# A planned FFN kernel on one core: transfers counted on a shared way, another order of the first loads, and the last pair's products in an order of their own

## The chip, the core and the metric

The kernel runs on one core of a Trainium2 chip. The metric is the device time of one execution in microseconds (us). A core has TensorE (PE, matrix products), VectorE (DVE), ScalarE (ACT), GpSimd (POOL) and SyncE (SP, which issues transfers here). Products accumulate in PSUM banks; everything else lies in SBUF. Every engine works through its own queue in the order in which its instructions were issued, and a semaphore makes it wait for another engine or a transfer.

## The reference, cut to what matters

```python
# x [64,64,1024], itok [64], cond weights [16,64,64]
W = weights[condition]                       # one 64x64 matrix per batch item
y = jnp.einsum('bct,bcd->bdt', x, W)         # mixes the 64 channels of an item
...
gate_logits = jnp.einsum('bsd,ed->bse', y, gate_w)          # 8 experts
weights, selected = jax.lax.top_k(gate_logits, 2)           # then softmax of the two
result = jnp.einsum('bsd,od->bso', y, base_w) + base_b      # 1024 -> 1024
low = jnp.einsum('bsd,erd->ebsr', y, lora_A)                # rank 16 for each expert
lora_out = jnp.einsum('ebsr,eor,bse->bso', low, lora_B, w_full)
result = result + 2.0 * lora_out
x = x + result
```

All values are float32.

## The kernel before, in words

There are 4,096 rows of 1,024 features, cut into 32 tiles of 128 rows (two batch items each). Mixing the channels acts on rows and the linear layers act on columns, so the kernel does the wide product first. It computes z = x * [lora_A | gate | base], 1,160 columns as three blocks of 388 (one padded), and then multiplies z from the left by the block-diagonal 128x128 matrix of the tile's two items. These second products are the `sums` (L431), into banks `ps_a` and `ps_o`.

Precision comes from splitting. Every f32 operand becomes a rounded high part (a CAST, L223, on ScalarE where nothing else is said) and a low part (operand minus high part, on VectorE, L220). A product of a row tile with one column block over 256 features is two halves of three matmuls (high x high, high x low, low x high), 128x388 each (`zstep`, L399).

The 16 pairs of row tiles come in two kinds. The first two (`NPLAIN`) run plainly: 24 products a pair (2 tiles x 3 column blocks x 4 stretches of features). The other 14 use a scheme with 20 products, p1 to p20, in the manner of Strassen's. Sums of x tiles (`sum_x`, L280) and of weight blocks (`mix_w`, L330) are formed once by VectorE, and then fewer products are needed. The products go to four banks, X, Y, R and Q (`ps_z0` to `ps_z3`); `BANK` (L61) says which. Partial results pass between them. `pass_on` (L690) is a ScalarE copy from one bank to another, times +1 or -1. `mix` (L707) is a VectorE add of a bank to a stored partial result `st`. p14, p15, p2, p8 and p9 all go to Y one after the other, and a mix stands after most of them.

When a chunk (one tile, one column block) of z is complete it is split (`zh`, `zl`), and `post` puts out the rest. For column block 0 this is the gate on the 8 logits, a transpose (L480) of the weighted low-rank part `low`, and its split `lth`/`ltl`. For all blocks it is the `sums`, with the matrix `bdr` gathered by POOL (L379) and with the LoRA products `lbh`, `lbl`. `finish` (L441) then adds to the token tile `xtok`, which holds x + bias. The token tile is loaded by SP (L365), and the bias is added by an accumulating transfer that POOL issues (L366). `store` writes it to memory, from POOL (L448), and for the last two tiles from SP (L450).

The order of nearly everything is planned. `Program.add` records a step with its engine, its cost and what it reads and writes. `Program.run` then lays the steps out greedily: on the engine that is free first, the ready step whose latest allowed start (`late`) is smallest. What it issues is in this planned order, on each engine. The planner knows hand-over times (`HOP`, `SAME`), when each engine may begin (`START`), and times after a step until its result counts as there (`lag`). In the kernel before, a load costs its bytes at 270 GB/s on SP, and `XLAG`, `WLAG`, `GATHER` and constants of 2, 4 and 5 us are its lags. TensorE's products alone have a fixed order (`PLAIN`, then `ORDER` made of `HEAD` and `TAIL`), and due times from it.

At the start the first weight block `b11` comes in two halves on ScalarE's queue, outside the plan (L301). The other blocks (`load_w`, L313) and the x tiles (`load_x`, L265) come on SP's queue, and `SUMS` forms weight sums as soon as their blocks are there. `b13` to `b43` are third-column blocks. The LoRA matrix `lb` is loaded into `xtok[2]` and split at L571 and L572.

Of the kernel before, what the change touches and what calls it, by code (L numbers as in the profile page):

```python
# [20 lines left out]
P = 128  # L21
B, C, T = 64, 64, 1024
NCOND = 16
E, R = 8, 16
# [18 lines left out]

HOP = {PE: 0.2, ACT: 0.15, DVE: 0.15, POOL: 0.15, SP: 1.0}
SAME = {PE: 0.0, ACT: 0.1, DVE: 0.12, POOL: 0.1, SP: 1.0}
START = {PE: 0.0, ACT: 2.0, DVE: 0.8, POOL: 1.7, SP: 1.4}
GATHER = 8.0
XLAG, WLAG = 3.0, 2.0
DMA = 1 / 270e3
AHEAD = 10.0  # L50
# [14 lines left out]
TAIL = ("p14", "p15", "p2", "p8", "p9")  # L65

SPLITS = (("f6", "a11"), ("s", "f5"), ("f19", "a22"), ("f11", "f13"), ("f18", "a24"), ("f3", "f1"), ("a13", "f9"),
          ("r", "f15"), ("f2", "f8"))
# [3 lines left out]
class Program:  # L72
# [6 lines left out]

    def add(self, engine, cost, fn, reads=(), writes=(), due=None, first=False, lag=0.0, early=None, port=False):  # L80

        n = len(self.steps)
        engine, cost = (e if isinstance(e, (list, tuple)) else [e] for e in (engine, cost))
        deps = set()
        for b in list(reads) + list(writes):
            if b in self.writer:
                deps.add(self.writer[b])
        for b in writes:  # L90
            deps.update(self.readers.get(b, ()))
        for b in reads:
            self.readers.setdefault(b, []).append(n)
        for b in writes:
            self.writer[b], self.readers[b] = n, []
        deps.discard(n)
        self.steps.append(dict(eng=dict(zip(engine, cost)), fn=fn, deps=deps, first=first, lag=lag, port=port,
                               due=self.horizon if due is None else due,
                               early=SP in engine and not reads if early is None else early))

    def run(self):
# [17 lines left out]
        def offer(i):  # L119
            for e in steps[i]["eng"]:  # L120
                t = max([0.0] + [end[d] + hop(by[d], e) + steps[d]["lag"]
                                 for d in steps[i]["deps"]])
                if steps[i]["early"]:
                    t = max(t, late[i] - AHEAD)
                t += MARGIN if steps[i]["first"] else 0.0
                cand[e].add((i, t))

        for i in range(n):
            if not left[i]:
                offer(i)  # L130
        done, port = 0, 0.0
        while done < n:
# [11 lines left out]
            end[i], by[i] = t + steps[i]["eng"][e], e  # L144
            free[e] = end[i]
            if steps[i]["port"]:
                port = end[i]
# [10 lines left out]
def cond_ffn_kernel(ctx, tc, xT, x, idx, cw, wall, bias, lb, out):  # L158
# [103 lines left out]

    def load_x(i, k, u, lag=XLAG):

        add(SP, DMA * 8 * P * P, lambda e: nc.sync.dma_start(  # L265
            xr[:, u].rearrange("p (k n) -> p k n", k=2), xT[i][:, 2 * k:2 * k + 2]), writes=[("xr", u)], lag=lag)

# [29 lines left out]


    raw["b11"] = Block("w_b11")
    for f in range(2):  # L300
        nc.scalar.dma_start(raw["b11"].ap()[:, f:f + 1], wall[0][0][:, f:f + 1])  # L301
    begun = [True]
    warm = sb.tile([P, 8], F32, name="warm")
    nc.vector.memset(warm, 0.0)
    nc.scalar.activation(warm, warm, AF.Exp)

    def load_w(m):

        k, n = int(m[1]) - 1, int(m[2]) - 1
        begun = m in raw  # L310
        if not begun:
            raw[m] = Block(f"w_{m}")
        add(SP, DMA * 8 * P * W, lambda e, b=raw[m]: None if begun else nc.sync.dma_start(b.ap(), wall[k][n]),  # L313
            writes=raw[m].keys, early=False)

# [10 lines left out]
    def mix_w(o, a, b, f, over):  # L326

        x, y = raw[a], raw[b]
        raw[o] = r = raw.pop(over) if over else Block(f"w_{o}")
        add(DVE, tt_cost(2 * W), lambda e: nc.vector.tensor_tensor(r.ap(), x.ap(), y.ap(), f),  # L330
            [k for z in (x, y) if z is not r for k in z.keys], r.keys, port=True)

# [29 lines left out]
    def load_tok(i):  # L362
        j = i % 3
        keys = [("xtok", j, c) for c in range(3)]
        add(SP, DMA * 4 * T * P, lambda e: nc.sync.dma_start(xtok[j], x[i * P:(i + 1) * P, :]), writes=keys, lag=4.0)  # L365
        add(POOL, 1.1, lambda e: nc.gpsimd.dma_start(xtok[j], bias.broadcast_to([P, T]), accum_op=ALU.add),  # L366
            writes=keys, lag=5.0)

    def late_sum(i):

        j = i % 3
        for src in (x[i * P:(i + 1) * P, :], bias.broadcast_to([P, T])):
            add(POOL, 1.1, lambda e, src=src: nc.gpsimd.dma_start(xtok[j], src, accum_op=ALU.add),
                writes=[("xtok", j, c) for c in range(3)], lag=5.0)

    def load_cond(i):
# [4 lines left out]
            in_offset=bass.IndirectOffsetOnAxis(ap=rows[:, i:i + 1], axis=0)),  # L381
            ["rows"], [("bdr", j)], lag=GATHER, early=True)
        add(ACT, 0.28, lambda e: copy(e, bdh[j], bdr[j]), [("bdr", j)], [("bdh", j)])
# [33 lines left out]

    def sums(i, c, b, q=None, part=(), with_lora=False, start=False, stop=False, first=True):

# [7 lines left out]
        def f(e):  # L427
# [5 lines left out]
        add(PE, len(part) * mm_cost(n) + 3 * with_lora * mm_cost(s.stop - s.start), f, sorted(names, key=str), [b],  # L433
            first=first)

# [8 lines left out]
    def store(i, cs):  # L444
        o, j = slice(outs(cs[0])[1].start, outs(cs[-1])[1].stop), i % 3
        src = [("xtok", j, c) for c in cs]
        if i < NT - 2:
            add(POOL, 1.0, lambda e: nc.gpsimd.dma_start(out[i * P:(i + 1) * P, o], xtok[j][:, o]), src, lag=2.0)  # L448
        else:
            add(SP, 0.5, lambda e: nc.sync.dma_start(out[i * P:(i + 1) * P, o], xtok[j][:, o]), src)  # L450

# [25 lines left out]
    def tr(i, b):  # L477
# [3 lines left out]
                                                  stop=False, skip_group_check=True),  # L481
            [("low", i % 2), "ident"], [b], first=True)
        add(ACT, 0.25, lambda e: copy(e, h, tp), [b], [("lth", i % 2)])
# [4 lines left out]
    def post(i, c, q):  # L488
# [7 lines left out]
        else:  # L496
            b = f"o{take('o', 2)}"
            if (i, c) == (NT - 2, 2):
                sums(i, c, b, with_lora=True, start=True)
                sums(i, c, b, q, (0, 1), first=False)  # L500
                sums(i, c, b, q, (2,), stop=True, first=False)
            else:
                sums(i, c, b, q, (0, 1, 2), True, True, True)
# [7 lines left out]
    for q in range(1, NPLAIN):  # L511
        PLAIN += [(i, c, k) for c in range(3) for i in (2 * q, 2 * q + 1) for k in range(KQ)]
    t = 4.2
    for i, c, k in PLAIN:
# [5 lines left out]
    for q in range(NPLAIN, NPAIR):  # L520
        nxt = HEAD if q + 1 < NPAIR else ()
        mixed = ("p14", nxt[0:1], "p15", nxt[1:2], "p2", nxt[2:3], "p8", "p9", nxt[3:])
# [20 lines left out]
    def load_split_x(i, k, **how):  # L543
        u = xrs.one()
        load_x(i, k, u, 0.0)
        xa0[i, k], = split_x([u], **how)
        xrs.give(u)

    for k in range(KQ):
        for i in range(2):  # L550
            load_split_x(i, k, hi=DVE if i == k == 0 else ACT)
            load_split_w(f"b{k + 1}{i + 1}", step=1 if i == k == 0 else 2)

# [14 lines left out]
    lraw = [("xtok", 2, c) for c in range(3)]  # L568
    add(SP, DMA * 4 * T * P, lambda e: nc.sync.dma_start(xtok[2], lb), writes=lraw)

# [108 lines left out]
    class Pair:  # L679
        def __init__(self, q):  # L680
            self.q, self.ops, self.at = q, Operands(q), {}

# [25 lines left out]

        def chunk(self, i, c, o):
            u = self.at[o]  # L710
            post(2 * self.q + i, c, split_z(CN[c], lambda: unit(u)[:, :CN[c]], ukey(u)))
            sts.give(u)

        def product(self, p):
            q, j, b = self.q, self.ops.split(p), BANK[p]
            for f in range(2):
                zstep((q, p, f), BANKS[b], j, p, f, p in OPENS and f == 0, p in STOPS and f == 1)
            self.ops.done(p)
            minus = ALU.subtract
            if p == "p6":  # L720
# [12 lines left out]
            elif p == "p13":  # L733
                self.mix("c23", "R", "p6")
                sts.give(self.at["p6"])
            elif p == "p18":
# [8 lines left out]
            elif p == "p12":  # L745
                post(2 * q, 0, split_z(N0, lambda: bank[BANKS["X"]][:, :N0], BANKS["X"]))
            elif p == "p14":
                self.mix("c23", "Y", "c23")
                self.chunk(1, 2, "c23")
            elif p == "p15":  # L750
                self.mix("c22", "Y", "c22")
                self.chunk(1, 1, "c22")
                store(2 * q + 1, range(3))
            elif p == "p2":
                self.mix("c12", "Y", "c12")
                self.chunk(0, 1, "c12")
                if q == NPAIR - 1:
                    store(2 * q, (0, 1))
            elif p == "p9":
                self.mix("c13", "Y", "c13", minus)  # L760
                self.chunk(0, 2, "c13")
                store(2 * q, (2,) if q == NPAIR - 1 else range(3))

# [51 lines left out]
```

## Time and profile before

| | |
|---|---|
| median of 3 runs | 467.27 us (466.59 to 467.89) |
| the profiled execution | 467.18 us |
| its span, first to last instruction | 465.2 us |
| VectorE: splits (L220), x and weight sums, partial results | 387.6 us busy |
| TensorE's first product / its last one starts | 5.06 / 460.30 us |
| last add on VectorE ends | 461.24 us |
| bytes moved | 75.00 MB, 161 GB/s on average |

The span leaves out about 2.0 us of the execution that lie before its first and behind its last instruction. The groups of instructions that the change touches most are these:

```profile
L280 DVE TENSOR_TENSOR xr<-xr 128x256 f32<-128x256 f32 (+1 forms) x139 | 71.1, 527 | 3.9 <-DMA xr<-in_xT 3.6
...
L690 ACT ACTIVATE ps_z<-ps_z 128x388 f32<-128x388 f32 x42 | 20.1, 480 | 31.7 <-PE ps_z L399 28.5
...
xr<-in_xT SPq DMA_DIRECT2D x128, 128.0 KB, 3.4
...
xtok<-in_x SPq DMA_DIRECT2D x28, 512.0 KB, 4.6
```

A group's line gives the code line, the engine, the operation, output <- input and how often; then its busy time and the mean of one in ns; then how long the engine had been idle just before and who ended most of that. A line of a transfer gives KB each and the median time from issue to landing. In a timeline the first number is the start in us, the second the duration, and brackets hold the idle time before and its releaser.

### The profile page before, as it was taken

How to read it: one execution, taken by the hardware profiler on the slowest of the kernel's cores; microseconds unless marked ns; L12 is line 12 of the kernel's file. 1: busy time of each engine (PE TensorE's matmuls, PEld its weight loads, DVE VectorE, ACT ScalarE, POOL GpSimd, SP SyncE). 2: the span in 40 equal slices, each digit the busy share in tenths (PEclk: the TensorE clock that was granted, in tenths of full speed). 3: DMA queues.
4: the chain of work that ended last, by engine and by line, in shares of the span. 5: the costliest groups of instructions: out<-in, count | busy, mean ns of one | idle time of the engine just before them, and what ended most of it. 6: DMA issues, size and time to landing. Idle time of an engine off the chain costs nothing.

```text
span 465.2 us, 7574 instructions
## 1 busy us (share of the span) xinstructions
PE 455.1 (98%) x2615; PEld 449.3 (97%) x2615; DVE 387.6 (83%) x938; ACT 223.2 (48%) x520; POOL 90.4 (19%) x107
## 2 busy tenths in 40 slices
PE   7999999999999999999999999999999999999986
PEld 6999999899999999999999999999999999999975
DVE  5999997788888898797888988888888889798573
ACT  5665665463643536364361735436363443636340
POOL 4020202413112021211303021120302203203200
PEclk9999999999999999999999999999999999999999
DMA  8940846884746556483576456476454646657542
GB/s 291 308 131 25 146 126 136 233 205 150 195 156 183 126 185 145 143 196 99 197 160 192 126 165 163 132 190 188 141 144 152 167 112 182 155 194 167 128 126 90
DMA packets 35509, 75.00 MB, mean 161 GB/s; under 512 B 4352, under 2 KB 21136, under 8 KB 35472
## 3 DMA queue, kind: packets, MB, share of 16 engines
q0 software_dynamic: 10560, 36.72, 33.4%
q1 hardware_dynamic: 24624, 37.41, 24.6%
q10 hardware_dynamic: 288, 0.40, 0.3%
q8 instruction: 20, 0.33, 0.3%
q14 instruction: 17, 0.14, 0.1%
HBM read 57.74 MB, written 16.78 MB: 160 GB/s over the span
## 4 chain that ended last, share of the span: by engine, by line
PE 91%; DMA 4%; DVE 2%; ACT 1%; issue 1%; SPq 0%; ACTq 0%; DVEq 0%
PE ps_z L399 70%; PE ps_o L431 14%; PE ps_a L431 6%; DMA xr<-in_xT 3%; DMA w_b<-in_w 1%; PE ps_a L480 1%; DVE st L707 1%; DVE xr L280 1%; DVE xl L220 0%; ACT st L223 0%; DVE xtok L441 0%; DVE wl_b_b L220 0%; SPq L265 0%; ACT wh_t_p L223 0%; ACT wh_b_b L223 0%
## 5 line engine op out<-in xcount | busy, mean ns | idle before, releaser
L223 ACT CAST xh<-xr 128x512 fp32r<-128x512 f32 (+1 forms) x137 | 82.9, 608 | 65.9 <-PE ps_z L399 64.8
L399 PE MATMUL ps_z<-wh_t_p,xh 128*128 128x388 f32 x308 | 105.6, 343 | 1.4 <-DVE st L707 1.3
L399 PE MATMUL ps_z<-wh_t_p,xl 128*128 128x388 f32 x308 | 104.3, 339 | 0.0
L399 PE MATMUL ps_z<-wl_t_p,xh 128*128 128x388 f32 x308 | 104.3, 339 | 0.0
L220 DVE TENSOR_TENSOR xl<-xr,xh 128x512 fp32r<-128x512 f32 (+1 forms) x138 | 92.0, 670 | 11.3 <-ACT xh L223 10.8
L707 DVE TENSOR_TENSOR st<-ps_z,st 128x388 f32<-128x388 f32 x126 | 70.4, 559 | 19.0 <-PE ps_z L399 14.8
L280 DVE TENSOR_TENSOR xr<-xr 128x256 f32<-128x256 f32 (+1 forms) x139 | 71.1, 527 | 3.9 <-DMA xr<-in_xT 3.6
L399 PE MATMUL ps_z<-wh_b_p,xh 128*128 128x388 f32 x180 | 62.3, 346 | 0.7 <-DVE st L707 0.7
L399 PE MATMUL ps_z<-wh_b_p,xl 128*128 128x388 f32 x180 | 61.0, 339 | 0.0
L399 PE MATMUL ps_z<-wl_b_p,xh 128*128 128x388 f32 x180 | 60.9, 338 | 0.0
L399 PEld LDWEIGHTS ps_z<-wh_t_p,xh 128*128 128x128 f32 x308 | 57.9, 188 | 3.1 <-DVE st L707 2.7
L399 PEld LDWEIGHTS ps_z<-wl_t_p,xh 128*128 128x128 f32 x308 | 57.9, 188 | 0.0
L399 PEld LDWEIGHTS ps_z<-wh_t_p,xl 128*128 128x128 f32 x308 | 57.8, 188 | 0.0
L448 POOL DMA_DIRECT2D out<-xtok x30 | 17.0, 566 | 186.8 <-DVE xtok L441 162.6
L223 ACT CAST zh<-st 128x388 fp32r<-128x388 f32 (+1 forms) x70 | 36.2, 517 | 34.1 <-DVE st L707 25.0
L366 POOL DMA_DIRECT2D xtok<-in_bias x28 | 25.6, 915 | 99.6 <-DMA xtok<-in_x 91.8
L379 POOL DMA_INDIRECT bdr<-in_cw,rows x32 | 38.8, 1212 | 26.0 <-DVE bdl L220 16.4
L441 DVE TENSOR_TENSOR xtok<-ps_o,xtok 128x388 f32<-128x388 f32 x56 | 31.4, 560 | 14.9 <-PE ps_o L431 14.2
L220 DVE TENSOR_TENSOR zl<-st,zh 128x388 fp32r<-128x388 f32 (+1 forms) x70 | 38.9, 555 | 4.4 <-ACT zh L223 4.1
L399 PEld LDWEIGHTS ps_z<-wh_b_p,xh 128*128 128x128 f32 x180 | 33.8, 188 | 2.1 <-DVE st L707 0.9
L690 ACT ACTIVATE ps_z<-ps_z 128x388 f32<-128x388 f32 x42 | 20.1, 480 | 31.7 <-PE ps_z L399 28.5
L399 PEld LDWEIGHTS ps_z<-wl_b_p,xh 128*128 128x128 f32 x180 | 33.8, 188 | 0.0
(130 smaller groups left out, 870.8 us busy)
## 6 DMA issues: line engine op xcount, KB each, us to landing
xr<-in_xT SPq DMA_DIRECT2D x128, 128.0 KB, 3.4
xtok<-in_bias POOLq DMA_DIRECT2D x32, 512.0 KB, 5.9
out<-xtok POOLq DMA_DIRECT2D x30, 512.0 KB, 3.1
xtok<-in_x SPq DMA_DIRECT2D x28, 512.0 KB, 4.6
w_b<-in_w SPq DMA_DIRECT2D x11, 388.0 KB, 5.7
xtok<-in_x POOLq DMA_DIRECT2D x4, 512.0 KB, 5.5
bdr<-in_cw,rows POOLq DMA_INDIRECT x32, 3.2
xtok<-in_lb SPq DMA_DIRECT2D x1, 512.0 KB, 4.7
```

The lines of the kernel that those rows point to most:

```text
L220: eng[e].tensor_tensor(o, a, b.bitcast(F32), ALU.subtract)
L223: (nc.scalar.copy if e == ACT else nc.vector.tensor_copy)(o, a)
L280: add(DVE, tt_cost(2 * P * len(os)), lambda e: nc.vector.tensor_tensor(some(xr, os), some(xr, xs), some(xr, ys), f), [("xr", u) for u in s ...
L366: add(POOL, 1.1, lambda e: nc.gpsimd.dma_start(xtok[j], bias.broadcast_to([P, T]), accum_op=ALU.add), writes=keys, lag=5.0)
L379: add(POOL, 1.04, lambda e: nc.gpsimd.indirect_dma_start(out=bdr[j], out_offset=None, in_=cw, in_offset=bass.IndirectOffsetOnAxis(ap=rows[ ...
L399: nc.tensor.matmul(z, l[:, j, n], w.ap()[:, f], start=(start and q == 0), stop=(stop and q == 2), skip_group_check=True)
L431: nc.tensor.matmul(d, l, r, start=(start and m == 0), stop=(stop and m == len(mms) - 1), skip_group_check=True)
L441: add(DVE, 0.09 + 0.00104 * (s.stop - s.start), lambda e: nc.vector.tensor_tensor(xtok[j][:, o], bank[b][:, s], xtok[j][:, o], ALU.add), [ ...
L448: add(POOL, 1.0, lambda e: nc.gpsimd.dma_start(out[i * P:(i + 1) * P, o], xtok[j][:, o]), src, lag=2.0)
L480: add(PE, 0.107, lambda e: nc.tensor.matmul(tp, low[i % 2][:, :ER], ident, is_transpose=True, start=False, stop=False, skip_group_check=True),
L690: add(ACT, 0.2 + 0.00085 * W, lambda e: nc.scalar.mul(z[b], z[x], scale), [BANKS[x]], [BANKS[b]])
L707: add(DVE, 0.09 + 0.00104 * W, lambda e: nc.vector.tensor_tensor(unit(u), a(), b(), f), reads, [ukey(u)])
```

## The change

The planner's picture of transfers is replaced. Before, SP was busy for as long as its bytes take, and fixed lags followed. Now issuing costs 0.45 us, each transfer has a `size`, and all transfers on whatever queue share one `wire`: one ends no sooner than 2.0 us after its issue, and no sooner than the one ahead of it plus its own bytes at 360 GB/s. In the backward pass a transfer counts as 5.0 us plus its bytes. `START` and SP's hand-over times are smaller. `after` lets a step begin no sooner than a given time. This alone moves steps of every engine over the whole kernel, since the plan is made anew.

The start: `b11` is loaded within the plan; `b12` is loaded in two halves too; for the first stretch of features both row tiles get their high parts on VectorE and the blocks are split in halves; and no weight sum begins before 11 us of the plan.

The last pair: its products follow an order of their own (`FINAL`) instead of `HEAD` and then `TAIL`; the sums of the last two tiles are divided in three steps each; and each finished chunk is stored by itself (6 stores in place of 3). For all pairs a chunk is posted as soon as the products it needs are done, and the buffer of p6 is given back when its last reader has run.

Instructions, before and after: TensorE 2,656 and 2,656, VectorE 876 and 880, ScalarE 524 and 524, POOL 112 and 112, SP 173 and 177.

```diff
-HOP = {PE: 0.2, ACT: 0.15, DVE: 0.15, POOL: 0.15, SP: 1.0}
-SAME = {PE: 0.0, ACT: 0.1, DVE: 0.12, POOL: 0.1, SP: 1.0}
-START = {PE: 0.0, ACT: 2.0, DVE: 0.8, POOL: 1.7, SP: 1.4}
-GATHER = 8.0
-XLAG, WLAG = 3.0, 2.0
-DMA = 1 / 270e3
+HOP = {PE: 0.2, ACT: 0.15, DVE: 0.15, POOL: 0.15, SP: 0.1}
+SAME = {PE: 0.0, ACT: 0.1, DVE: 0.12, POOL: 0.1, SP: 0.1}
+START = {PE: 0.0, ACT: 0.74, DVE: 0.8, POOL: 1.7, SP: 0.75}
+ISSUE = 0.45
+FLIGHT, DMA = 2.0, 1 / 360e3
+QUEUE = 3.0
+FIRST = 11.0
+TWICE = 2.5
...
+FINAL = ("p6 p16 p7 p5 p19 p17 p14 p11 p13 p18 p3 p4 p20 p10 p12 p15 p2 p1 p8 p9").split()
...
-        self.steps.append(dict(eng=dict(zip(engine, cost)), fn=fn, deps=deps, first=first, lag=lag, port=port,
+        self.steps.append(dict(eng=dict(zip(engine, cost)), fn=fn, deps=deps, first=first, size=size, port=port,
+                               lag=FLIGHT + QUEUE + size * DMA if size else 0.0, after=after,
...
-                t = max([0.0] + [end[d] + hop(by[d], e) + steps[d]["lag"]
-                                 for d in steps[i]["deps"]])
+                t = max([steps[i]["after"]] + [end[d] + hop(by[d], e) for d in steps[i]["deps"]])
...
+            if steps[i]["size"]:
+                end[i] = wire = max(end[i] + FLIGHT, wire) + steps[i]["size"] * DMA
...
+        b = raw[m] = Block(f"w_{m}")
+        if k == 0 and n < 2:
+            for f in range(2):
+                q, dma = (SP, nc.sync.dma_start) if n else (ACT, nc.scalar.dma_start)
+                add(q, ISSUE, lambda e, f=f, dma=dma: dma(b.ap()[:, f:f + 1], wall[k][n][:, f:f + 1]),
+                    writes=b.keys[f:f + 1], size=4.0 * P * W, early=False)
...
-            [k for z in (x, y) if z is not r for k in z.keys], r.keys, port=True)
+            [k for z in (x, y) if z is not r for k in z.keys], r.keys, port=True, after=FIRST)
...
-        add(SP, DMA * 4 * T * P, lambda e: nc.sync.dma_start(xtok[j], x[i * P:(i + 1) * P, :]), writes=keys, lag=4.0)
+        add(SP, ISSUE, lambda e: nc.sync.dma_start(xtok[j], x[i * P:(i + 1) * P, :]), writes=keys, size=4.0 * T * P)
...
-            first=first)
+            first=i < NT - 2)
...
-            if (i, c) == (NT - 2, 2):
+            if i >= NT - 2:
                 sums(i, c, b, with_lora=True, start=True)
-                sums(i, c, b, q, (0, 1), first=False)
-                sums(i, c, b, q, (2,), stop=True, first=False)
+                sums(i, c, b, q, (0, 1))
+                sums(i, c, b, q, (2,), stop=True)
...
-    t = 4.2
+    t = 4.9
...
-        nxt = HEAD if q + 1 < NPAIR else ()
+        if q == NPAIR - 1:
+            break
+        nxt = HEAD if q + 2 < NPAIR else FINAL
...
-            load_split_x(i, k, hi=DVE if i == k == 0 else ACT)
-            load_split_w(f"b{k + 1}{i + 1}", step=1 if i == k == 0 else 2)
+            load_split_x(i, k, hi=DVE if k == 0 else ACT)
+            load_split_w(f"b{k + 1}{i + 1}", step=1 if k == 0 else 2)
...
+            self.out.add((i, c))
+            if self.q == NPAIR - 1:
+                store(t, (c,))
+            elif all((i, c) in self.out for c in range(3)):
+                store(t, range(3))
...
+            for i, c, o, need in ((1, 2, "c23", "p13 p14 p20"), (1, 1, "c22", "p1 p15 p20"),
+                                  (0, 1, "c12", "p3 p2 p12"), (0, 2, "c13", "p9 p12")):
+                if p in need.split() and set(need.split()) <= self.done:
+                    self.chunk(i, c, o)
```

## The prediction

> **What bounds the kernel now.** First the page: how busy each engine is, and the chain of work that ended last.
>
> ```profile
> PE 455.1 (98%) x2615; PEld 449.3 (97%) x2615; DVE 387.6 (83%) x938; ACT 223.2 (48%) x520; POOL 90.4 (19%) x107
> ...
> PEclk9999999999999999999999999999999999999999
> ...
> PE 91%; DMA 4%; DVE 2%; ACT 1%; issue 1%; SPq 0%; ACTq 0%; DVEq 0%
> ```
>
> TensorE works for 455.1 of 465.2 us at its full clock. The built program after the change issues the same 2,656 TensorE rows, only in another order. So the work stays, and only TensorE's pauses and the two ends of the span can change. Next I read its waits in stretches.
>
> ```profile
> PE ps_z L399 <- DVE xl L220: 1.1, 1, 1.1
> ...
> PE ps_z L399 <- DVE st L707: 0.9, 2, 0.7
> ...
> PE ps_z L399 <- DVE st L707: 1.9, 3, 0.7
> ```
>
> These come from 0 to 20 us, from 60 to 94 and from 430 to the end. From 94 to 430 the same view is empty. There are three places to win, each with its own reason, and 336 us in which there is something to lose and nothing to win.
>
> **The start.** The timeline from 0 to 10 us:
>
> ```profile
> 7.16 1.05 DVE L330 TENSOR_TENSOR w_w<-w_b,w_b 128x776 f32<-128x776 f32 x1
> ...
> 8.14 0.95 DVE L220 TENSOR_TENSOR wl_b_b<-w_b,wh_b_b 128x776 fp32r<-128x776 f32 x1
> ...
> 9.01 0.41 DVE L220 TENSOR_TENSOR xl<-xr,xh 128x256 fp32r<-128x256 f32 x1
> ...
> 9.48 0.44 PE L399 MATMUL ps_z<-wh_b_b,xl 128*128 128x388 f32 x1 [1.11 <-DVE xl L220]
> ```
>
> The ninth matmul needs the low part of the second row tile. VectorE makes it only after a weight sum (1.05) and a split of a whole block (0.95). From 9.48 on TensorE runs without a gap. After the change no weight sum runs before the scheduler's 11 us, and VectorE's order is: high part of tile 0, half block, low part of tile 0, high part of tile 1, half block, low part of tile 1. When can these begin? Rates in slices of 0.35 us:
>
> ```profile
> GB/s 0 0 0 0 0 79 109 56 56 362 356 412 399 408 389 377 419 381 393 334 301 367 387 368 428 417 393 391 404 402 381 400 416 405 351 420 363 349 375 373
> ```
>
> Both x tiles and the first block are 131 + 131 + 397 = 659 KB. The row adds up to 640 KB at 4.55 us. The first tile and half block (330 KB, there by 3.8) were first used at 4.21, so about 0.4 us passes from landing to use; all three are usable by 5.05. VectorE is free of tile 0's low part at 5.84 (5.42 + 0.42). It then needs 0.29 (high part), 0.56 (half block) and 0.42 (low part): 5.84 + 1.27 = 7.1. With 0.1 to 0.25 us for hand-overs (9.01 + 0.41 to 9.48 is 0.06) the ninth matmul starts at about 7.35. Gain 9.48 - 7.35 = 2.13. The sums and the whole-block splits cost the same later: VectorE keeps its 71.1 us of L280 sums and 92.0 us of splits.
>
> Something comes back. The load of the LoRA matrix (512 KB) and three x tiles now stand before the last third-column weight block on SP's queue, and the split of that block and of the LoRA matrix (1.08 us on ScalarE, 1.22 on VectorE) stand in front of the low part of the second output bank. My walk through the new order, with row durations 0.84 (high part of a block), 0.95 (low part), 0.52 and 0.55 (same for a bank), ends it at 28.05; TensorE, 2.1 us earlier, wants the bank at 27.55. I take 0.55 lost. Bounds: 0 (the LoRA split falls behind) and 1.5 (it and one more x split fall in front). Net start **1.6**, bounds 0.6 to 2.1.
>
> **The first pair of the twenty-product scheme.** The timeline around 84 us:
>
> ```profile
> 83.55 0.43 DVE L280 TENSOR_TENSOR xr<-xr 128x256 f32<-128x256 f32 x1 [2.18 <-DMA xr<-in_xT]
> ...
> 84.50 0.56 DVE L707 TENSOR_TENSOR st<-ps_z,st 128x388 f32<-128x388 f32 x1
> ...
> 85.57 0.55 DVE L707 TENSOR_TENSOR st<-st,ps_z 128x388 f32<-128x388 f32 x1
> ...
> 86.17 0.44 PE L399 MATMUL ps_z<-wh_t_p,xh 128*128 128x388 f32 x1 [0.69 <-DVE st L707]
> ```
>
> VectorE stood 2.18 us at a sum of x tiles whose load was late. Behind it in its queue were the mixes that free TensorE's banks, so TensorE lost 0.85 us here (this wait and slower issue around it) and 0.35 more at 92.99. In the new order that sum is issued behind both mixes. The stall should go: **+0.9** of the 1.2. But a 512 KB token load now stands in SP's queue between the x loads this pair still wants. Before, four x loads (4 x 131 KB) took 8.3 us here, 63 GB/s, beside POOL's accumulating loads; token loads of 512 KB took 2.4 and 1.9 us in quieter stretches. So bounds +1.2 and -2.0.
>
> **94 to 430 us.** Same products, VectorE four instructions more in all (876 to 880: 0.335 x 2 against 0.6 for a divided sum, 0.2 us together), no wait there now. I counted VectorE's work in front of each of TensorE's waits in both orders; the slack differs by up to 2 us either way and stays positive. I take 0. The cover is that slack: VectorE is 83% busy, and a late x load of over 2 us would end it.
>
> **The last pair.** The timeline from 448 us, and the stores' issues:
>
> ```profile
> 448.64 0.44 PE L399 MATMUL ps_z<-wh_h_p,xh 128*128 128x388 f32 x1 [0.66 <-DVE st L707]
> ...
> 451.14 0.44 PE L399 MATMUL ps_z<-wh_b_p,xh 128*128 128x388 f32 x1 [0.55 <-DVE st L707]
> ...
> 453.12 0.44 PE L399 MATMUL ps_z<-wh_t_p,xh 128*128 128x388 f32 x1 [0.65 <-DVE st L707]
> ```
>
> ```profile
> out<-xtok SPq DMA_DIRECT2D x1, 318.0 KB, 2.4
> out<-xtok SPq DMA_DIRECT2D x1, 194.0 KB, 2.8
> ```
>
> p15, p2, p8 and p9 all write bank Y, and each product must wait until VectorE has added the one before (0.56 plus hand-overs: about 0.82 each time, 3 times = 2.5). p12 ends at 446.24; from there 11.4 us of matmuls (65 of 0.1757) take until 460.3, and the last add ends at 461.24: 15.0 us. The new order puts two sums between p15 and p2, and p1 between p2 and p8, 1.05 us of other work or more each, which covers the 0.82. One new wait takes their place: p3 follows p18 directly on bank X, and ScalarE must first copy that bank (0.48 a copy, about 0.8 with hand-overs); before, p4 and p20 stood between. At the end the transpose, its copy (0.27) and the LoRA sums cost 0.65 once. My walk gives 12.9 us from the same point to the last add: gain 2.1, less 0.8 for p18 to p3, net **1.3**, bounds 0.5 (one bank wait returns) and 1.8 (half the new wait is covered). The stores get smaller, 194 KB each, the last two issued 0.47 us apart. Before, 194 KB landed 2.8 us after its issue and 318 KB 2.4, so from the last add to the end (3.9 us) I change nothing.
>
> A rule speaks against this division. The Trainium skill, "DMA: Bandwidth & Descriptors", section "Anatomy of one DMA — SWDGE (gpsimd) path", gives every transfer some 2.0 us fixed beside bytes / 436 GB/s, and its section "Bandwidth" asks for a MiB and more in each. By that figure, an estimate, three more stores would cost up to 6 us if each waited for the one before. In the trace the last store's packets began at 462.57, before the last packet of the one ahead had ended (462.72), so fixed parts overlap, and by the row the division costs nothing.
>
> **Sum.** The profiled execution took 467.18 (span 465.2 and 2.0 outside it), 0.09 from the median of 467.27. 467.18 - 1.6 - 0.9 - 0 - 1.3 = **463.4**.
>
> **Rivals.**
> A, the forecast: 463.4, its own range 461.9 to 465.0. Chance 0.54.
> B, the early lead is lost in the first 95 us: the first pair waits for x loads whose pace the queue sets, so TensorE only arrives earlier at the same wait. Then the tail alone is left: 467.18 - 1.3 = 465.9. For: the 2.18 us wait is on a DMA, not on VectorE. Against: buffers free earlier too, so loads start earlier. Chance 0.18.
> C, slower: the token load in SP's queue takes its 512 KB at 47 to 63 GB/s, the rate of this stretch, 8.3 to 11 us, and the two x loads behind it hold up a sum and its products by 3.7 to 6.5 us. At 6.5: 463.4 + 6.5 = 469.9. It decides for slower once the load takes over some 8.4 us (all of 3.8 gained is gone). Against: 2.4 and 1.9 us for such loads a little later. Chance 0.13.
> D, nothing comes back: 2.1 + 1.2 + 1.8 = 5.1, 462.1. Chance 0.15.
>
> **How the numbers follow.** A measurement of this kernel tells 0.3%, 1.4 us, from no change: faster below 465.9, slower above 468.7. A and D are faster, B sits on the border (a third of it faster), and C spreads from 467 up, a third of it within: faster 0.54 + 0.15 + 0.05 = 0.74, same 0.14, slower 0.12. The range leaves out the far end of C and of D: 461.5 to 467.0.
>
> **What would show it.** Start: the ninth matmul near 7.35, no L330 sum ahead of it, and one TensorE wait on VectorE's zl near 27.5. First pair: no wait on L707 at 84 to 86; a VectorE sum that waits some us for a load at 88 to 92 would be C. Middle: the list stays empty; any wait there falsifies the 0. End: one wait of 0.6 to 0.8 on ScalarE between p18 and p3, none on L707 at Y, 3.9 us from last add to end. The forecast is wrong if the ninth matmul is early and the first pair is not (B), or if waits appear after 94.

## The result and the profile after

The changed kernel takes **462.40 us** (median of five executions; 461.63 to 464.09) against 467.27 before: a ratio of 0.990, 95% interval 0.9877 to 0.9923. The profiled execution took 461.99 us with a span of 460.0, 5.2 us shorter than before.

In 32 of the 85 executions of the kernels with the whole old start (before, e1, e6, e8) the mean granted clock of TensorE was 0.990 to 0.996, in none of the 54 of the other kernels, and the profiled execution of e8 is of these (0.50 from 9 to 14 us), which cost it 2.2 us by matmul 180, so its leads are read as differences after that point.

The page of the changed kernel, first its busy times:

```profile
PE 453.2 (99%) x2615; PEld 449.5 (98%) x2615; DVE 381.2 (83%) x942; ACT 225.5 (49%) x520; POOL 91.8 (20%) x107
```

TensorE does the same 2,615 recorded matmuls in about the same busy time, and the span has closed up around it. Where the pauses went is in its waits, from 0 to 20 us and then from 430 us to the end. From 20 to 430 the list is empty.

```profile
PE ps_z L407 <- ACT wh_b_b L230: 0.2, 1, 0.2
...
PE ps_z L407 <- ACT ps_z L702: 0.6, 1, 0.6
PE ps_o L439 <- ACT lth L230: 0.2, 1, 0.2
```

(Lines have moved: L399 is now L407, L707 is L719, L690 is L702, L280 is L288.) The wait of 1.1 us on `xl` and all waits on the mixes are gone; one wait on ScalarE's copy of a bank has come.

To see where the time was won, I put the n-th matmul of one trace beside the n-th of the other. Outside the small sums and the last pair they are the same work. The count is from 0 and begins with the 39 warm-up matmuls; times are from the start of the span. The lead is the start time before minus the start time after:

| matmul | before, us | after, us | lead |
|---|---|---|---|
| 48 (early) | 9.76 | 7.50 | 2.27 |
| 180 | 33.05 | 31.15 | 1.90 |
| 480 | 85.15 | 83.24 | 1.91 |
| 540 | 97.13 | 93.86 | 3.28 |
| 2340 | 410.34 | 406.24 | 4.10 |
| 2460 | 431.30 | 427.12 | 4.18 |
| 2520 | 441.45 | 438.39 | 3.06 |
| 2584 | 455.34 | 449.62 | 5.72 |
| last | 460.30 | 455.08 | 5.22 |

So: 1.9 net at the start, 1.4 in the first pair of twenty products, 0.8 to 0.9 spread over 330 us of the middle, and 1.0 to 1.1 in the last pair.

The start, in the timeline of the changed kernel:

```profile
5.68 0.29 DVE L230 CAST xh<-xr 128x256 fp32r<-128x256 f32 x1
...
5.88 0.57 DVE L227 TENSOR_TENSOR wl_b_b<-w_b,wh_b_b 128x388 fp32r<-128x388 f32 x1
...
6.38 0.50 DVE L227 TENSOR_TENSOR xl<-xr,xh 128x256 fp32r<-128x256 f32 x1
...
7.32 0.34 PE L407 MATMUL ps_z<-wh_b_b,xl 128*128 128x388 f32 x1
```

VectorE makes high part, half block and low part one behind the other. The ninth matmul, the one at 7.32, waits for nothing any more. A little comes back near 28 us, where the low part of the second bank (`zl`) is late as TensorE wants the bank:

```profile
27.32 0.55 DVE L227 TENSOR_TENSOR zl<-ps_z,zh 128x384 fp32r<-128x384 f32 x1
...
27.93 0.19 PEld L407 LDWEIGHTS ps_z<-wh_b_b,xh 128*128 128x128 f32 x1 [0.32 <-DVE zl L227]
```

In the first pair of twenty products the two mixes now run on time, and the sums of x tiles stand behind them:

```profile
81.58 0.56 DVE L719 TENSOR_TENSOR st<-ps_z,st 128x388 f32<-128x388 f32 x1
...
82.55 0.56 DVE L719 TENSOR_TENSOR st<-st,ps_z 128x388 f32<-128x388 f32 x1 [0.42 <-PE ps_z L407]
...
85.17 1.15 DVE L288 TENSOR_TENSOR xr<-xr 128x256 f32<-128x256 f32 x2
```

VectorE waits for the banks (0.42 on TensorE), no longer for a load. The last pair, by timeline and by the issues of its stores:

```profile
437.75 0.44 PE L407 MATMUL ps_z<-wh_t_p,xh 128*128 128x388 f32 x1 [0.58 <-ACT ps_z L702]
...
450.13 0.44 PE L439 MATMUL ps_o<-lbh,lth 128*128 128x388 f32 x1 [0.24 <-ACT lth L230]
...
455.28 1.03 DVE L449 TENSOR_TENSOR xtok<-ps_o,xtok 128x388 f32<-128x388 f32 x2 [0.72 <-PE ps_o L439]
```

```profile
out<-xtok SPq DMA_DIRECT2D x4, 194.0 KB, 2.2
out<-xtok SPq DMA_DIRECT2D x2, 124.0 KB, 1.9
```

p3 waits for ScalarE's copy of bank X, the only wait between products. The last add ends at 456.31, 4.93 us earlier than before, and the span at 459.96, 3.65 us later (3.92 before).

### The profile page after: what moved, and what is told of

The parts are those of the page before. It is cut to its first block, busy times and chain, and to the rows that moved or that the text cites. A ratio compares the mean times of both kernels' runs of the same rounds, so it can differ in the third digit from the quotient of the medians.

```text
span 460.0 us, 7554 instructions
## 1 busy us (share of the span) xinstructions
PE 453.2 (99%) x2615; PEld 449.5 (98%) x2615; DVE 381.2 (83%) x942; ACT 225.5 (49%) x520; POOL 91.8 (20%) x107
## 5 line engine op out<-in xcount | busy, mean ns | idle before, releaser
L407 PE MATMUL ps_z<-wh_t_p,xh 128*128 128x388 f32 x308 | 105.9, 344 | 0.6 <-ACT ps_z L702 0.6
L407 PE MATMUL ps_z<-wl_t_p,xh 128*128 128x388 f32 x308 | 104.4, 339 | 0.0
L407 PE MATMUL ps_z<-wh_t_p,xl 128*128 128x388 f32 x308 | 104.3, 339 | 0.0
L719 DVE TENSOR_TENSOR st<-ps_z,st 128x388 f32<-128x388 f32 x126 | 70.2, 558 | 24.7 <-PE ps_z L407 23.3
L288 DVE TENSOR_TENSOR xr<-xr 128x256 f32<-128x256 f32 (+1 forms) x141 | 71.1, 520 | 7.1 <-DMA xr<-in_xT 7.0
L407 PE MATMUL ps_z<-wh_b_p,xh 128*128 128x388 f32 x180 | 61.4, 341 | 0.0
L407 PE MATMUL ps_z<-wh_b_p,xl 128*128 128x388 f32 x180 | 61.1, 339 | 0.0
L407 PE MATMUL ps_z<-wl_b_p,xh 128*128 128x388 f32 x180 | 60.9, 339 | 0.0
L407 PEld LDWEIGHTS ps_z<-wh_t_p,xh 128*128 128x128 f32 x308 | 57.8, 188 | 1.7 <-ACT ps_z L702 0.9
L407 PEld LDWEIGHTS ps_z<-wl_t_p,xh 128*128 128x128 f32 x308 | 57.9, 188 | 0.0
L407 PEld LDWEIGHTS ps_z<-wh_t_p,xl 128*128 128x128 f32 x308 | 57.9, 188 | 0.0
L702 ACT ACTIVATE ps_z<-ps_z 128x388 f32<-128x388 f32 x42 | 20.1, 478 | 67.8 <-PE ps_z L407 67.8
L387 POOL DMA_INDIRECT bdr<-in_cw,rows x32 | 40.0, 1251 | 25.7 <-DVE zl L227 12.7
L407 PEld LDWEIGHTS ps_z<-wh_b_p,xh 128*128 128x128 f32 x180 | 33.8, 188 | 0.1
L407 PEld LDWEIGHTS ps_z<-wl_b_p,xh 128*128 128x128 f32 x180 | 33.8, 188 | 0.0
```

Source lines behind the costliest of these rows:

```text
L288: add(DVE, tt_cost(2 * P * len(os)), lambda e: nc.vector.tensor_tensor(some(xr, os), some(xr, xs), some(xr, ys), f), [("xr", u) for u in s ...
L387: add(POOL, 1.04, lambda e: nc.gpsimd.indirect_dma_start(out=bdr[j], out_offset=None, in_=cw, in_offset=bass.IndirectOffsetOnAxis(ap=rows[ ...
L407: nc.tensor.matmul(z, l[:, j, n], w.ap()[:, f], start=(start and q == 0), stop=(stop and q == 2), skip_group_check=True)
L702: add(ACT, 0.2 + 0.00085 * W, lambda e: nc.scalar.mul(z[b], z[x], scale), [BANKS[x]], [BANKS[b]])
L719: add(DVE, 0.09 + 0.00104 * W, lambda e: nc.vector.tensor_tensor(unit(u), a(), b(), f), reads, [ukey(u)])
```

## The experiments

Times are medians, with the ratio to the kernel before on the same chip and its interval. The four experiments of a group ran on one chip: e1 to e4 beside 467.19 for the kernel before, e5 to e8 beside 467.11, the last four beside 466.51.

**e1: the old start back.**

```diff
-FIRST = 11.0
+FIRST = 0.0
-        if k == 0 and n < 2:
+        if k == 0 and n < 1:
-            load_split_x(i, k, hi=DVE if k == 0 else ACT)
-            load_split_w(f"b{k + 1}{i + 1}", step=1 if k == 0 else 2)
+            load_split_x(i, k, hi=DVE if i == k == 0 else ACT)
+            load_split_w(f"b{k + 1}{i + 1}", step=1 if i == k == 0 else 2)
```

> The changed kernel with its start as before: weight sums from time 0 of the plan, the second row tile's first high part on ScalarE, its block in one piece. Theory (the start gave 1.9 of the 4.9 us): the ninth matmul is back near 9.5 us, and the time is 1.5 to 2.3 us above the changed kernel's, some 464.3. Rival (the lead of the start would have been had later anyway, because what follows is paced by loads): the ninth matmul is late but the time stays within 0.7 us of the changed kernel's.

Measured 465.07 (0.9962, 0.9942 to 0.9981), 2.7 above the changed kernel. The ninth matmul started at 9.62. Against the changed kernel TensorE was 2.40 us behind at matmul 48, 1.96 at 180 and 2.95 at 540. So the start is worth 1.9 to 2.0 up to there, as the theory has it. The rest is a stall in the first pair, where again a sum and a load stand before the mixes:

```profile
84.84 0.43 DVE L288 TENSOR_TENSOR xr<-xr 128x256 f32<-128x256 f32 x1 [0.30 <-DMA xr<-in_xT]
...
85.65 0.55 DVE L719 TENSOR_TENSOR st<-st,ps_z 128x388 f32<-128x388 f32 x1
...
86.25 0.45 PE L407 MATMUL ps_z<-wh_t_p,xh 128*128 128x388 f32 x1 [0.54 <-DVE st L719]
```

The new start changes the plan of the next 80 us too, and that part of its worth was not expected (1.5 to 2.3 us were).

**e2: the last pair in the old order.**

```diff
-        if q == NPAIR - 1:
-            break
-        nxt = HEAD if q + 2 < NPAIR else FINAL
+        nxt = HEAD if q + 1 < NPAIR else ()
```

> The changed kernel with the last pair in the order of all other pairs (HEAD, then TAIL); the divided sums and the six stores stay. Theory (the order of products is what the tail gave): the three waits on L719 at bank Y return, 0.55 to 0.7 us each, the wait of p3 on ScalarE goes, and the time rises by 1.0 to 1.8 us, to some 463.8. Rival (the stores and the finer sums gave the gain of the end): within 0.5 us of the changed kernel, with the distance from the last add to the end shorter than the 3.9 us of before.

Measured 463.73 (0.9927, 0.9905 to 0.9950), 1.3 above the changed kernel, as the theory expects. Its waits from 430 us on:

```profile
PE ps_z L407 <- DVE st L717: 1.2, 2, 0.7
PE ps_o L439 <- DVE xtok L449: 0.2, 1, 0.2
```

Two waits on bank Y are back (not three), and the wait on ScalarE is gone. The order of products makes the gain of the end, not the stores or the finer sums, which stayed.

**e3: the old planner with the new start and the new last pair.** The kernel before with the lines of the start and of `FINAL`, `Pair` and `sums` taken over:

```diff
+FIRST = 11.0
...
-                t = max([0.0] + [end[d] + hop(by[d], e) + steps[d]["lag"]
+                t = max([steps[i]["after"]] + [end[d] + hop(by[d], e) + steps[d]["lag"]
...
+        if m == "b12":
+            b = raw[m]
+            for f in range(2):
+                add(SP, DMA * 4 * P * W, lambda e, f=f: nc.sync.dma_start(b.ap()[:, f:f + 1], wall[k][n][:, f:f + 1]),
+                    writes=b.keys[f:f + 1], early=False)
+            return
```

> The kernel before with the new start and the new last pair, but its old planner of transfers (fixed lags, 270 GB/s on SP). Theory (the planner alone moved VectorE's sum of x tiles behind the mixes in the first pair of twenty products): that stall is back, TensorE waits for L719-like mixes near 82 to 91 us for 0.9 to 1.4 us in all, and the time is 1.0 to 2.0 us above the changed kernel's, some 464. Rival (the earlier start alone dissolved the stall, the planner is worth nothing): no TensorE wait between 60 and 94 us, and the time within 0.5 us of the changed kernel's.

Measured 464.79 (0.9941, 0.9921 to 0.9961), 2.4 above the changed kernel and 2.4 below before. From matmul 180 to 360 its trace is level with the changed kernel's (within 0.04 us). Then it loses 1.06 in the first pair (by matmul 540), at the old stall, though everything comes 1.9 us earlier:

```profile
81.77 0.42 DVE L284 TENSOR_TENSOR xr<-xr 128x256 f32<-128x256 f32 x1 [2.20 <-DMA xr<-in_xT]
...
82.71 0.55 DVE L719 TENSOR_TENSOR st<-ps_z,st 128x388 f32<-128x388 f32 x1
...
83.78 0.55 DVE L719 TENSOR_TENSOR st<-st,ps_z 128x388 f32<-128x388 f32 x1
...
84.39 0.44 PE L409 MATMUL ps_z<-wh_t_p,xh 128*128 128x388 f32 x1 [0.72 <-DVE st L719]
```

The sum waits 2.20 us here and 2.18 before: the load moved forward with the work around it, and the lead carried nothing away. After this pair it loses another 1.4 us by matmul 2340. Beside the new start and the new last pair the planner is worth 2.4 us, more than the 1.0 to 2.0 expected, and more than half of it in the middle.

**e4: p4 ahead of p3 in the last pair.**

```diff
-FINAL = ("p6 p16 p7 p5 p19 p17 p14 p11 p13 p18 p3 p4 p20 p10 p12 p15 p2 p1 p8 p9").split()
+FINAL = ("p6 p16 p7 p5 p19 p17 p14 p11 p13 p18 p4 p3 p20 p10 p12 p15 p2 p1 p8 p9").split()
```

> The changed kernel with one exchange in the last pair: p4 runs before p3, so that ScalarE's copy of bank X after p18 has a product of 1.05 us beside it. Theory (the wait of p3 on L702 is uncovered and at the end of the chain): the wait of 0.58 us near 437.8 is gone and the time falls by 0.5 to 0.75 us. Rival (the time goes to a wait behind it, at p20 to p10 or at the last sums): the wait is gone, another of 0.3 us or more stands behind it, and the time stays within 0.25 us.

Measured **461.26** (0.9866, 0.9844 to 0.9887; 460.84 to 462.13), 1.1 below the changed kernel's 462.40. All that is left from 430 us on in its waits:

```profile
PE ps_o L439 <- ACT lth L230: 0.2, 1, 0.2
```

Between matmul 2340 and 2520 it gains 0.85 us on the changed kernel's trace, more than the 0.58 in the wait's line, since the pause there was 0.84 of issue time (two gaps of 0.91 and 0.28 in place of 0.1757 each). Elsewhere the profiled execution lost 0.4 us: a weight load waited 0.42 us for a mix at 363.46, where the changed kernel, with the same order of products, has no wait. At the last matmul it is 0.43 ahead. This is the fastest kernel of the study by its median. Its interval overlaps the changed kernel's, so that the size is not settled and the sign rests on the vanished pause.

**e5: the new start alone**, on the kernel before (the edit of e3 without `FINAL`, `Pair` and `sums`).

> The kernel before with the new start alone (weight sums from 11 us, halves, high parts on VectorE). Theory (the start is worth 1.9 us once the later give-back is paid, and the stall of the first pair is the planner's): ninth matmul near 7.6, TensorE still waits 0.5 to 0.9 us for a mix in the first pair of twenty products, time 465.2 (1.6 to 2.3 below before). Rival (the lead carries the stall away with it): no such wait, and 464.4 or less.

Measured 465.50 (0.9953, 0.9933 to 0.9972), 1.6 below before. The ninth matmul started at 7.71, the lead was 1.69 at matmul 180, and the wait on a mix in the first pair stayed (0.8). The theory holds, the rival falls: a lead does not dissolve that stall. In the trace the lead goes from 1.93 at matmul 540 to 1.34 at 2340, so the new start gains nothing in the middle by itself.

**e6: the new last pair alone**, on the kernel before.

> The kernel before with the new last pair alone (order of products, divided sums, six stores). Theory (the tail gives 1.0 to 1.4 net, independent of the rest): 465.9, with one TensorE wait of 0.6 us on ScalarE's copy of bank X in place of three on the mixes. Rival (the tail's gain needs the new planner, which puts gathers, token loads and sums in time): less than 0.5 us below before, with a wait on bdr, xtok or a low part behind the last product.

Measured 466.25 (0.9976, 0.9957 to 0.9995), 0.9 below before. In its trace the lead over before goes from 0.03 at matmul 2340 to 1.31 at the last one, a gain of 1.28. Its only larger wait from 430 us on is the expected one on ScalarE (0.7). The tail needs nothing of the planner.

**e7: three stores in place of six.**

```diff
-            if self.q == NPAIR - 1:
-                store(t, (c,))
+            if self.q == NPAIR - 1 and i == 0:
+                if c == 2 or all((i, c) in self.out for c in range(2)):
+                    store(t, (2,) if c == 2 else (0, 1))
```

> The changed kernel with the stores of the last pair grouped as before (318, 512 and 194 KB in place of six). Theory (transfers of a queue overlap in their fixed part, so the division costs nothing and sends the first bytes earlier): the time is the same within 0.4 us, from the last add to the end 3.5 to 3.9 us in both. Rival, the rule of 2.0 us for each transfer: three transfers fewer make the end 1 to 6 us earlier.

Measured 462.07 (0.9877, 0.9851 to 0.9903). That is the same time as with six. From the last add (457.69) to the end of the span (461.7) it takes 4.0 us, against 3.65 with six in the changed kernel. That difference tells nothing: over all traces it is 3.25 to 4.38 with six and 3.75 to 4.0 with three. Six stores do not pay a fixed part six times over. In the changed kernel the last two were issued at 455.87 and 456.34 and landed at 457.99 and 458.63, 0.64 us apart. The Trainium skill ("DMA: Bandwidth & Descriptors", section "Anatomy of one DMA — SWDGE (gpsimd) path") gives some 2.0 us fixed for a transfer that GpSimd issues. These are issued by SP, and a fixed part of that size does not add up for transfers that stand behind one another in this queue.

The profiled execution had lost 1.2 us to the changed kernel before the last pair, on the same order of instructions there:

```profile
89.01 0.43 DVE L288 TENSOR_TENSOR xr<-xr 128x256 f32<-128x256 f32 x1 [1.58 <-DMA xr<-in_xT]
```

In the changed kernel this sum ran at 87.28 with no wait. Here the token load ahead of the loads still due took 5.9 us by its packets (80.00 to 85.89) and not 4.5, and two products then waited 0.3 us each for a mix (at 91.44 and 94.14). So the arrival of loads there differs from one execution to the next. It fits the risk that the prediction saw in the token load; what held that load up is not shown.

**e8: the late sum held back in the kernel before.** Step 504 of the plan is the sum that waits 2.18 us.

```diff
-                t = max([0.0] + [end[d] + hop(by[d], e) + steps[d]["lag"]
+                t = max([84.0 if i == 504 else 0.0] + [end[d] + hop(by[d], e) + steps[d]["lag"]
```

> The kernel before with one step held back in the plan: the sum of x tiles that waits 2.18 us for its load may begin only after 84 us of the plan, which puts it behind the two mixes that it blocked; what follows that pair is planned anew. Theory (the mixes were only queued behind a waiting instruction): the waits of 0.69 and 0.19 us on L707 near 86 and 93 us are gone, and the lead over before at the end of the first pair is 0.8 to 1.2 us. Rival (the loads are the limit): the wait moves to a product on the sum's low part, and the lead stays under 0.3 us.

Measured 467.18 (0.9998, 0.9977 to 1.0018): no gain. Of the two waits in the first pair the large one is gone. The small one stays, about 2 us later than before:

```profile
94.91 0.42 PE L399 MATMUL ps_z<-wh_b_p,xh 128*128 128x388 f32 x1 [0.27 <-DVE st L707]
```

TensorE's lead over before rises by 0.73 us there (-2.66 to -1.93), a little less than expected. But it falls by 0.27 between matmul 900 and 1260, and by 0.55 between 2160 and 2340, where the plan that follows is a new one. The cause of the large pause is shown. The small one does not go with that step. Three other sums of x tiles stand ahead of its mix (from 92.45 us), and whether they make it was not tested. That the removal of the stall alone is worth its length is refuted: what a new plan does further on weighs as much.

**The changed kernel again**, for the last group.

> The changed kernel unchanged, for a comparison on the same chip with the three below: 462.4, no TensorE wait between 20 and 430 us.

Measured 462.06 (0.9898, 0.9878 to 0.9918). Its trace runs 0.1 to 0.2 us ahead of the first one from matmul 180 to the last.

**e9: weight sums allowed early.** `FIRST = 0.0` alone.

> The changed kernel with weight sums allowed from the start of the plan; the halves and the high parts on VectorE stay. The first weight sum then stands behind the low part of the second row tile, not before it. Theory (the order of VectorE's first eight steps makes the 2.1 us, not the ban on sums): ninth matmul near 7.3, time within 0.6 us of the changed kernel. Rival (the 1.05 us sum only moves in front of the next block's split): a TensorE wait of 0.5 to 1.1 us on a wl or xl between 7.5 and 12 us, and 462.9 to 463.5.

Measured 462.07 (0.9894, 0.9874 to 0.9914), the same as the changed kernel. The ninth matmul started at 7.12. The ban on early sums does nothing here; the halves and the high parts on VectorE put the low part ahead by themselves.

**e10: the ban without the halves.** The edits of e1 except `FIRST`.

> The changed kernel with the ban on early sums, but the second block in one piece and the second tile's high part on ScalarE as before. Theory (each step ahead of the low part costs its own duration): only the whole split (0.95) stands ahead, the ninth matmul starts near 8.4, and the time is 0.8 to 1.2 us above the changed kernel's. Rival (the arrival of the whole 397 KB block sets it): 9.0 us or later, and 1.5 us or more above.

Measured 463.82 (0.9935, 0.9918 to 0.9952), 1.8 above the changed kernel of the same group. The ninth matmul started at 8.57 (8.4 expected): VectorE's whole split took 0.97 and stood ahead of the low part. That cost 1.36 at matmul 48 and 0.98 at 180. Then 1.0 more went in the first pair, by a wait of 0.5 on a mix. The time expected was too low by that stall.

**e12: the late sum pulled forward in the changed kernel.**

```diff
-                t += MARGIN if steps[i]["first"] else 0.0
+                t = 81.46 if i == 509 else t + (MARGIN if steps[i]["first"] else 0.0)
```

> The changed kernel with one step pulled forward in the plan of the first pair of twenty products: the sum of x tiles that waits for its load goes in front of the two mixes on VectorE, as it stood in the kernel before. Its load landed at 84.96 us in the changed kernel. Theory (a waiting instruction at the head of VectorE's queue holds the mixes, and TensorE behind them): VectorE waits 2 us or more for that load, TensorE waits 1.5 to 3.2 us for L719 near 83 to 87 us, and the time is 1.2 to 3.2 us above the changed kernel's. Rival (e8's result: such a stall is won back later, since something else limits): the wait is there, but the time rises by less than 0.5 us.

Measured 463.44 (0.9935, 0.9912 to 0.9957), in two clusters: 462.52 to 462.61 and 464.28 to 465.27; the median is 1.4 above the changed kernel of the same group. The profiled execution is of the lower one. Its timeline at this place:

```profile
80.84 0.69 DVE L227 TENSOR_TENSOR xl<-xr,xh 128x512 fp32r<-128x512 f32 x1 [1.48 <-ACT xh L230]
81.95 0.42 DVE L288 TENSOR_TENSOR xr<-xr 128x256 f32<-128x256 f32 x1 [0.41 <-DMA xr<-in_xT]
82.29 0.68 DVE L227 TENSOR_TENSOR xl<-xr,xh 128x512 fp32r<-128x512 f32 x1
82.89 0.55 DVE L719 TENSOR_TENSOR st<-st,ps_z 128x388 f32<-128x388 f32 x1
```

The expectation was wrong in its number. I had taken the wrong load for this sum: its own landed at 81.85 (81.74 in the changed kernel), and a split already stood before it. VectorE waited 0.41 and TensorE lost 0.3 us. In the upper cluster the load may have come later, as another did in e7; that was not seen in a trace and stays open.

## Why the prediction was right, point by point

**The start** (2.13, less 0.55, net 1.6) was right. The ninth matmul came at 7.32 where 7.35 was worked out, a gain of 2.16. By matmul 48 the lead was 2.27, and 0.37 of it came back by matmul 180, at the place and on the `zl` that were named; the two short pauses at 27.6 and 27.9 hold 0.26 of it. Net 1.9. One reason was wrong in part: the weight sum's removal and the new order were told as one, but e9 shows that the order alone does it, and e10 that the ban alone gives 1.05 (9.62 in e1 to 8.57) and leaves 1.25.

**The first pair** (0.9 of 1.2, bounds +1.2 and -2.0) had the right mechanism, and its size was low. The trace shows 1.38: the two pauses before were 0.96 and 0.42 of issue time, and the bracketed waits, by which I had counted, leave out the slow restart behind each. That the order of VectorE's queue makes the large pause is shown by e3 (the order of the old planner, the same wait of 2.20) and by e8 (that one step moved, the pause gone). What ended the small one was not tested by itself: in e8 it is still there (0.51 of issue time), in e3 it is not. The planner does not do it alone either: with the old start (e1) or with half of the new one (e10), 1.0 of the 1.38 is lost again. The counter-risk, the token load ahead of two x loads, did not bite in the profiled execution: by the trace's DMA packets it took 4.5 us (79.94 to 84.44), half of rival C's 8.3, and the loads behind it landed at 86.58 and 89.32 with no wait on VectorE for any load from 60 to 100 us. In e7's execution a sum did wait for a load there, which cost 1.2 us, so its absence here is in part luck.

**The middle** (0) is the step that failed, by 0.8 to 0.9 us. The prediction said that the wait list from 94 to 430 us was empty and that any wait there would falsify the 0; the list stayed empty and the 0 was wrong all the same. It was empty before too, for matmuls, but the list of the weight loads' waits of the kernel before is not:

```profile
PEld ps_z L399 <- DVE st L707: 0.7, 3, 0.4
```

For the changed kernel that list is empty. Of the 0.8, one pause at 306.3 holds 0.33 (two gaps of 0.40 and 0.28 in place of 0.1757 each). In this stretch seventeen transposes stood between two products before and fourteen after, at 0.47 us from the matmul ahead to the second one behind against 0.41 beside small sums: 3 x 0.06 = 0.18. The rest is spread over many intervals and was not located. That the gain is the planner's is shown by e3 (1.4 is lost here without it), e5 and e6 (no gain here from the start or the last pair alone); e8 shows that a plan can lose 0.8 here as well.

**The last pair** (2.1 less 0.8, net 1.3) was right in its mechanism, and its sum lies near by some luck. The profile has 1.1, e2 1.3 and e6 0.9 to 1.3. Of the 1.1, only 0.8 was there at the last add (a lead of 4.93 against 4.10 at matmul 2340), which is where the walk of the prediction ended; the other 0.27 came from the last add to the end, a distance that differs by more than that from trace to trace. The wait of p3 on ScalarE was 0.84 of issue time (0.8 predicted), and e4 shows it to be on the path.

**The sum.** In leads, 1.9 + 1.4 + 0.8 + 1.1 = 5.2 against 1.6 + 0.9 + 0 + 1.3 = 3.8, and 462.4 against 463.4. Rival D's number (462.1) lies nearer, by another reason: it gave nothing back and had nothing in the middle. Rival B falls: the lead of 1.9 was whole at matmul 480 and grew there. e5 and e3 show that B was right in one thing, the stall does come along with the lead, so the planner had to take it away. Two shares of the prediction do not follow from its own terms: two thirds of B and a third of C make 0.16 for "same" and leave 0.09 for "slower" (0.14 and 0.12 were given), and a token load of 8.4 us, which takes away all of the gain, would make the time the same and not slower.

**The stores.** The prediction set their division at nothing, against the page's rule. e7 bears it out: 462.07 with three, 462.40 and 462.06 with six. (The packet times that it gives, 462.57 and 462.72, are 462.32 and 462.47 from the start of the span; their order stands.)

## What to carry to other kernels

When an engine that is off the critical path stands at a late load, look at what is queued behind it: the order in its queue decides, not its load, and running the whole kernel earlier does not help, since the load moves along (2.18 and 2.20 us). An engine that is 98% busy is read at its restarts: compare the n-th instruction of two traces, and ask the weight loads' waits too, before a stretch is called free of waits. A hand-made order that removes one wait is worth a second look at the place where two uses of one bank have come together: here one exchange gave another 0.85 us at that place of the trace.

## What the runs showed of the hardware

A restart of TensorE costs more than the wait that a trace writes in brackets: 0.58 and 0.69 us in brackets were 0.84 and 0.96 us of lost issue time. A single 128x128 transpose between two products costs 0.06 us more than one that stands beside a small sum. Transfers in one queue overlap in their fixed part: three stores in place of six left the time as it was (462.07 against 462.06 and 462.40), and two that took 2.1 and 2.3 us from issue to landing landed 0.64 us apart. And the landing of loads beside POOL's accumulating transfers differs between executions of one order of instructions: the same 128 KB load, issued at 74.13 and 74.01 us, landed at 80.06 in one execution of the changed kernel and at 77.73 in another.
